# A graph layer whose fourth gather of each group takes 126 rows instead of 125

## The chip, the cores and the metric

The kernel runs on one core of a Trainium2 chip. The metric is the device time of one execution in microseconds (us). The engines of a core work side by side: TensorE (PE, with its weight loads PEld), VectorE (DVE), ScalarE (ACT), GpSimd (POOL) and SyncE (SP). Transfers are carried by 16 DMA engines; SP, ACT and POOL issue them.

## What is computed

One layer of a graph network over 12500 nodes of 64 features and 412500 edges of 32 features. The edges are sorted by receiver (`dst`), while their senders (`src`) are in no order.

```
h = relu(layernorm(x))
msg_in = concat(h[src], h[dst], edge_attr)                  # 160 wide
messages = silu(msg_in @ W1 + b1) @ W2 + b2
att      = softmax(silu(msg_in @ Wa1 + ba1) @ Wa2 + ba2)    # over all edges
aggregated = segment_sum(messages * att, dst)
x = x + (silu(concat(h, aggregated) @ Wu1 + bu1) @ Wu2 + bu2)
```

## The kernel before

**Tables.** The first phase (`gnn_kernel`, lines 90 to 313) normalises the nodes and multiplies them with the sender's and the receiver's part of the two first weight matrices. The products are kept in DRAM as two tables with a row of C = 128 floats (512 B) for each node: `ts_d` for senders, `tr_d` for receivers. An edge then needs the sum of a row of `ts_d`, a row of `tr_d` and a product of its own features.

**Groups and tiles.** `one_pass` (line 393) goes through the edges in NG = 413 groups of K = 8 tiles of EP = 125 edges; 3300 tiles hold all edges and the last four are padding. Within a tile each edge has its own partition, so partitions 125 to 127 are not used.

**The gather of senders.** `load(g)` (line 523) takes a buffer `gs` of 128 partitions x 8 x 128 floats from a pool of seven (line 161), keeps the first 125 partitions, and issues one indirect DMA on GpSimd for each tile (line 530). It reads 125 numbers of rows from one column of `src_sb` and fetches those rows of `ts_d` to partitions 0 to 124 of its eighth of the buffer. `src_full` (line 130) is the same table of row numbers with all 128 partitions; the host has padded partitions 125 to 127 with zeros. In 131 groups, the set `chosen` (every third group from 10 on), the eighth tile isn't gathered: ScalarE copies its 125 columns out of `hT` one by one (line 503) and TensorE multiplies them (line 565). That leaves 413 x 8 - 131 = 3173 gathers.

**The rest of a group.** Receivers are sorted, so a group's rows of `tr_d` lie in a window of 32 rows, loaded by SP (line 551). VectorE makes a one-hot matrix (line 555) and TensorE multiplies it and the edge features with the window (line 559). `begin(g)` adds the gathered rows (line 570) and ScalarE takes the tanh (line 573), from which VectorE forms the silu, the message and the attention logits (lines 583 to 594). Every four groups the largest logit is brought up to date. `by_node` (line 637) makes the weighted one-hot matrices, TensorE sums the messages by node (line 643), and `put` adds these sums to those kept in SBUF (lines 668 and 672) and notes the maximum they stand for (line 675).

**Order.** VectorE, ScalarE and TensorE follow the order in the code (`pin` keeps it). Loads run two groups ahead of their use. GpSimd's own order is that of the calls of `load`, with nothing else on it from the first gather to the last; each gather waits for the one eight before it, whose semaphore it shares, and for its buffer to be free. After the last group a short phase updates the nodes (from line 822).

Of the kernel before, what the change touches and what calls it, by code (L numbers as in the profile page):

```python
# [44 lines left out]
F32 = mybir.dt.float32  # L45
# [8 lines left out]
P = 128  # L54
EP = 125
# [3 lines left out]
C = 2 * U  # L59
S1 = U + 1  # L60
K = 8
# [13 lines left out]
PHASE = 1  # L75
SLOTS = (((0, 24), (24, 24)), ((48, 24), (72, 12)), ((84, 24), (108, 17)))
ROUND = 12582912.0
EPS = 1e-5
NEG = -3.0e38
BIG = 3.0e38  # L80
# [9 lines left out]
def gnn_kernel(ctx: ExitStack, tc: tile.TileContext, n_edges, x, src, src_row, dst, dst_row, first, edge,  # L90
# [73 lines left out]
    with tc.tile_pool(name="node1", bufs=1) as node1, \  # L164
# [41 lines left out]
        eps = node1.tile([P, 1], F32, name="eps")  # L206
        nc.vector.memset(eps, EPS)
        pin(nc.scalar.activation(node1.tile([P, 1], F32, name="spare"), eps, AF.Sqrt))
# [90 lines left out]
        for c, nn in chunks:  # L299
            tr = node.tile([P, CB, C], F32, name="tr")[:, :nn, :]  # L300
            for b in range(0, nn, 4):
                n = min(4, nn - b)
                pn = node_ps.tile([P, 4, C], F32, name="pn", bufs=4)
                for i in range(0, n, 2):
# [7 lines left out]
        pin(nc.scalar.dma_start(hT_d, hT))  # L312

    one_pass(tc, n_edges, locals())
    again = nc.values_load(wrong[0:1, 0:1], min_val=0, max_val=1,
                           skip_runtime_bounds_check_because="it is the outcome of a comparison")
# [76 lines left out]
def one_pass(tc, n_edges, v):  # L393
    nc = tc.nc
    NB, T, NG, NP, NT = (v[k] for k in ("NB", "T", "NG", "NP", "NT"))
    ident, iota_w, bj, dloc, src_sb, base_sb, real, unreal, far, wrong = (
        v[k] for k in ("ident", "iota_w", "bj", "dloc", "src_sb", "base_sb", "real", "unreal",
                       "far", "wrong"))
    ts_d, tr_d, bq_d, xb_d, edge, dst_row = (
        v[k] for k in ("ts_d", "tr_d", "bq_d", "xb_d", "edge", "dst_row"))  # L400
    wa2, ba2_c, w2b, wu1a, wu2h, we, gather = (
        v[k] for k in ("wa2", "ba2_c", "w2b", "wu1a", "wu2h", "we", "gather"))
# [8 lines left out]
    with ExitStack() as ctx:  # L411
# [38 lines left out]
        for w in wins:  # L450
            nc.vector.memset(w, 0.0)
            for r in range(2):
                rows = slice(WR + r * DE, WR + (r + 1) * DE)
                nc.vector.tensor_copy(w[rows, :, r, :], we[rows, None, :].to_broadcast([DE, 2, C]))
        with tc.tile_pool(name="work2", bufs=2) as work2, \
# [3 lines left out]
            pes, gss, lgs, ps_, psums, sps, pps, ees, mts, nums, cols = ({} for _ in range(11))  # L459
# [20 lines left out]
            def places(g):  # L480
# [7 lines left out]
                pin(nc.vector.tensor_scalar(near, to, 1.0 / m, 0.5 / m - 0.5, op0=ALU.mult, op1=ALU.add))  # L488
                pin(nc.vector.tensor_scalar(near, near, ROUND, None, op0=ALU.add))
                pin(nc.vector.tensor_scalar(near, near, ROUND, float(1 - m * P), op0=ALU.subtract, op1=ALU.mult))  # L490
                pin(nc.vector.scalar_tensor_tensor(to, to, float(P), near, op0=ALU.mult, op1=ALU.add))
# [13 lines left out]
            def burst(g, k):  # L505
                for i in range(EVERY):
# [6 lines left out]
                           ap=[[C, NP + WR - SHIFT], [SHIFT * C, 2], [1, C]])  # L513

            def registers(g, engine, at, base=base_sb, top=NP - 1):
                n = min(NQ, NG + (base is not base_sb) - g)
                _, regs = nc.values_load_multi_w_load_instructions(
                    base[0:1, g:g + n], engines=[engine], min_val=0, max_val=top,
                    skip_runtime_bounds_check_because=WHY)
                for i in range(n):  # L520
                    at[g + i] = regs[i]

            def load(g):

                t = g * K
                if g % NQ == 0:
                    registers(g, ENG.SP, at_sp)
                gs = gss[g] = gather.tile([P, K, C], F32, name="gs")[:EP]
                for j in range(K - (g in chosen)):
                    nc.gpsimd.indirect_dma_start(  # L530
                        out=gs[:, j, :], out_offset=None, in_=ts_d[:, :],
                        in_offset=bass.IndirectOffsetOnAxis(ap=src_sb[:, t + j:t + j + 1], axis=0))
                if g % NQ == 0:
                    n = min(NQ, NG - g) * E2
                    eo = eos[g // NQ % 2]
                    i = g // NQ % 2
                    db = dbs[i * WR:(i + 1) * WR].bitcast(I32)
                    for i in range(g, min(g + NQ, NG)):
                        e = slice((i - g) * E2, (i - g + 1) * E2)
                        ees[i] = eo[:, e], db[:, e]  # L540
                    nc.sync.dma_start(eo[WR:, :n],
                                      edge[:, g * E2:g * E2 + n])
                    for r in range(2):
                        nc.sync.dma_start(
                            db[r * R:(r + 1) * R, :n],
                            bass.AP(tensor=dst_row.tensor, offset=dst_row[r:r + 1, g * E2:].offset,
                                    ap=[[0, R], [1, n]]))
                eo, db = ees.pop(g)
                win = wins[g % WINS]
                for r in range(2):  # L550
                    nc.sync.dma_start(win[r * R:(r + 1) * R, :, r, :],
                                      tr_w[bass.ds(at_sp[g], R), :, :])
                for h in range(2):
                    e = slice(h * E2 // 2, (h + 1) * E2 // 2)
                    pin(nc.vector.tensor_scalar(eo[:WR, e], db[:, e], bj[g // NQ % 2 * WR:(g // NQ % 2 + 1) * WR, g, h:h + 1], None,  # L555
                                                op0=ALU.is_equal))
                pe = pes[g] = pre_ps.tile([P, K, C], F32, name="pe")[:EP]
                for q in range(H):
                    pin(nc.tensor.matmul(pe[:, 2 * q:2 * q + 2, :], eo[:, q * EP:(q + 1) * EP],  # L559
                                         win[:, q // 2, :, :], start=True,  # L560
                                         stop=q < H - 1 or g not in chosen))
                if g in chosen:
                    to, _ = cols[g]
                    pin(nc.vector.scalar_tensor_tensor(to, nums[g], half, to, op0=ALU.is_equal, op1=ALU.mult))
                    pin(nc.tensor.matmul(pe[:, K - 1, :], to, stack, start=False, stop=True))
# [166 lines left out]
            for g in range(AHEAD):  # L732
                load(g)
            done = 0
            for g in range(NG):
# [18 lines left out]
                if g + AHEAD < NG:  # L754
                    load(g + AHEAD)
# [382 lines left out]
```

## Time and profile before

| | |
|---|---|
| median of 3 runs | 4922.53 us (4922.45 to 4923.75) |
| the profiled execution | 4935.06 us |
| its span, first to last instruction | 4933.3 us |
| gathers (line 530) | 3173, first start 51.9 us, last start 4875.7 us |
| one gather, shortest / median / longest | 1207 / 1212 / 1726 ns |
| queue 0 (GpSimd's transfers) | 253840 packets, 206.77 MB |
| queue 1 (SP's transfers) | 121458 packets, 174.49 MB |

The profile is one execution, so sums of its durations are made against its own time, which is a little over the median of the runs. In a group's line the columns are the code line, the engine, the operation, output and inputs by the program's names, and the number of instructions; then busy time and mean duration, and the idle time of the engine just before them with what ended it. "issue" means that the engine waited for nothing the profile shows. In the view of one line, three durations stand for shortest, median and longest in ns. In the timeline the columns are start, duration, engine, line and operation, and idle time before it. A gather's duration on POOL is the time GpSimd works on it, not that of the transfer, which the DMA engines do afterwards.

### The profile page before, as it was taken

What the parts mean: (1) busy time and instruction counts of PE and PEld (TensorE: products, weight loads), DVE (VectorE), ACT (ScalarE), POOL (GpSimd) and SP (SyncE); (2) the same over time, 40 slices, a digit from 0 to 9 for tenths busy, and PEclk for the clock granted to TensorE, in tenths of its full rate; (3) what the DMA queues carried; (4) which work ended last, traced back from release to release, by engine and by line L of the source; (5) the groups of instructions that cost most, each with busy time, mean ns of one, the idle gap of its engine ahead of it and who ended that gap; (6) DMA issues with size and microseconds to landing.
All of it is one profiled execution on the core that took longest, in us unless ns stands there. A gap on an engine that the chain in (4) does not pass through costs nothing. (4 is left out here: it accounts for less than half of the span.)

```text
span 4933.3 us, 81829 instructions
## 1 busy us (share of the span) xinstructions
PE 2429.9 (49%) x11509; PEld 1950.7 (40%) x11509; DVE 3456.5 (70%) x9793; ACT 2214.0 (45%) x17625; POOL 3871.1 (78%) x3198
## 2 busy tenths in 40 slices
PE   5455555445544444544444544444445445444455
PEld 4343344334433333433333443333334334334344
DVE  6677777777776766766766776766767667667667
ACT  3444444444444444444444444444444444444412
POOL 4777877777777777777777777777777777777775
PEclk8666655665666665555665555566566666655655
DMA  7333333333333333333333333233333333333333
GB/s 248 76 76 83 87 75 82 89 74 83 81 75 76 71 74 76 70 75 76 69 76 76 68 76 76 68 76 76 69 76 71 74 76 70 75 76 70 75 91 81
DMA packets 377225, 396.20 MB, mean 80 GB/s; under 512 B 230333, under 2 KB 306039, under 8 KB 376290
## 3 DMA queue, kind: packets, MB, share of 16 engines
q0 software_dynamic: 253840, 206.77, 19.0%
q1 hardware_dynamic: 121458, 174.49, 14.9%
q10 hardware_dynamic: 1376, 9.67, 0.5%
q14 instruction: 457, 3.74, 0.3%
q8 instruction: 94, 1.54, 0.1%
HBM read 361.41 MB, written 25.72 MB: 78 GB/s over the span
## 5 line engine op out<-in xcount | busy, mean ns | idle before, releaser
L530 POOL DMA_INDIRECT gs<-ts_d,src_sb x3173 | 3853.9, 1215 | 1020.6 <-issue 962.4
L559 PE MATMUL pe<-wins,eo 128*125 128x256 f32 x3304 | 1524.4, 637 | 1551.2 <-DVE eo L555 1288.7
L503 ACT COPY cols<-hT 128x1 f32 x16375 | 1630.2, 189 | 754.3 <-issue 749.8
L559 PEld LDWEIGHTS pe<-wins,eo 128*125 128x125 f32 x3304 | 997.4, 319 | 1872.4 <-DVE eo L555 1375.5
L570 DVE TENSOR_TENSOR gs<-pe,gs 125x1024 f32<-125x1024 f32 (+1 forms) x413 | 487.5, 1180 | 1153.1 <-DMA gs<-ts_d,src_sb 1140.2
L573 ACT ACTIVATE pe<-gs 125x1024 f32<-125x1024 f32 x413 | 424.8, 1029 | 1768.2 <-DVE gs L570 859.2
L637 DVE TENSOR_SCALAR wt<-iota_w,dloc,p 125x40 f32<-125x40 f32 x3304 | 772.5, 364 | 1.8
L643 PE MATMUL sp<-wt,acts 125*65 125x40 f32 x6608 | 652.2, 270 | 13.2 <-DVE wt L637 9.2
L643 PEld LDWEIGHTS sp<-wt,acts 125*65 125x65 f32 x6608 | 612.5, 185 | 23.6 <-DVE wt L637 14.0
L613 PE MATMUL mt<-ident,mx 125*128 125x125 f32 x110 | 48.1, 438 | 644.7 <-DVE sums L672 608.1
L654 PEld LDWEIGHTS mt<-ss,w2u 65*128 65x128 f32 x826 | 210.7, 283 | 362.0 <-issue 235.4
L654 PE MATMUL mt<-ss,w2u 65*128 65x40 f32 x826 | 188.3, 322 | 262.8 <-DVE gm L620 199.4
L555 DVE TENSOR_SCALAR eo<-dbs,bj 64x250 f32<-64x250 int32 x826 | 303.2, 397 | 17.9 <-DMA dbs<-in_dst_row_dram 8.5
L591 DVE TENSOR_TENSOR pe<-pe,w_all 125x512 f32<-125x512 f32 x413 | 288.8, 699 | 13.7
L589 DVE SCALAR_TENSOR_TENSOR pe<-pe,gs 125x512 f32<-125x512 f32 x413 | 287.4, 696 | 10.8
L583 DVE SCALAR_TENSOR_TENSOR acts<-pe,gs 125x512 f32<-125x512 f32 x413 | 284.6, 689 | 12.8 <-issue 2.4
L594 DVE TENSOR_REDUCE lg<-pe 125x8 f32<-125x512 f32 x413 | 284.2, 688 | 10.8
L613 PEld LDWEIGHTS mt<-ident,mx 125*128 125x128 f32 x110 | 20.0, 182 | 655.8 <-issue 652.2
L675 DVE COPY stand<-nmax 64x40 f32 x826 | 217.1, 263 | 3.3
L672 DVE TENSOR_TENSOR sums<-sums,mt 64x40 f32 x606 | 114.4, 189 | 4.7 <-issue 0.4
L668 DVE SCALAR_TENSOR_TENSOR sums<-sums,scale,mt 64x40 f32 x220 | 55.8, 254 | 78.4 <-PE mt L654 59.6
L356 DVE TENSOR_SCALAR bu<-mt,w_all 64x256 f32<-64x256 f32 (+1 forms) x50 | 23.9, 478 | 92.6 <-PE mt L347 78.6
(124 smaller groups left out, 1123.2 us busy)
## 6 DMA issues: line engine op xcount, KB each, us to landing
eo<-in_edge_dram SPq DMA_DIRECT2D x103, 500.0 KB
dbs<-in_dst_row_dram SPq DMA_DIRECT2D x206, 250.0 KB
gs<-ts_d,src_sb POOLq DMA_INDIRECT x3173
wins<-tr_d SPq DMA_DIRECT2D x826, 32.0 KB
num<-in_src_row_dram SPq DMA_DIRECT2D x131, 62.5 KB
ts_d<-ts SPq DMA_DIRECT2D x5, 896.0 KB
tr_d<-tr ACTq DMA_DIRECT2D x5, 896.0 KB
hT_d<-hT ACTq DMA_DIRECT2D x1, 3136.0 KB
```

What stands on the lines that cost most here:

```text
L503: pin(nc.scalar.copy(to[:, first + i:first + i + 1], hT[:, bass.ds(regs[i], 1)]))
L530: nc.gpsimd.indirect_dma_start(out=gs[:, j, :], out_offset=None, in_=ts_d[:, :], in_offset=bass.IndirectOffsetOnAxis(ap=src_sb[:, t + j:t ...
L555: pin(nc.vector.tensor_scalar(eo[:WR, e], db[:, e], bj[g // NQ % 2 * WR:(g // NQ % 2 + 1) * WR, g, h:h + 1], None, op0=ALU.is_equal))
L559: pin(nc.tensor.matmul(pe[:, 2 * q:2 * q + 2, :], eo[:, q * EP:(q + 1) * EP], win[:, q // 2, :, :], start=True, stop=q < H - 1 or g not in ...
L570: pin(nc.vector.tensor_tensor(gss[g][:, :n, :], pes[g][:, :n, :], gss[g][:, :n, :], ALU.add))
L573: pin(nc.scalar.activation(pes[g], gss[g], AF.Tanh))
L583: pin(nc.vector.scalar_tensor_tensor(acts[g % ACTS][:, :, 0:U], th[:, :, U:C], 1.0, gs[:, :, U:C], op0=ALU.add, op1=ALU.mult))
L589: pin(nc.vector.scalar_tensor_tensor(att, th[:, :, 0:U], 1.0, gs[:, :, 0:U], op0=ALU.add, op1=ALU.mult))
L591: pin(nc.vector.tensor_tensor(att, att, wa2[:EP, None, :].to_broadcast([EP, K, U]), ALU.mult))
L637: pin(nc.vector.tensor_scalar(wt[:, j, :], iota_w[:EP, j // H, :], dloc[:, g * K + j:g * K + j + 1], p[:, k + j:k + j + 1], op0=ALU.is_equ ...
L643: pin(nc.tensor.matmul(sp, acts[g % ACTS][:, j, :], wt[:, j, :], start=j == 0, stop=j == K - 1))
L654: pin(nc.tensor.matmul(pp, w2u.rearrange("s h u -> s (h u)"), sps.pop(g), start=True, stop=True))
```

## The change

The constant `WIDE = 126` is new. The gather of tile 3 of each group (the fourth) now reads 126 row numbers and writes 126 partitions; the others stay at 125. The added row number lies in the padding of `src_full` and is 0, so the added row is row 0 of `ts_d`, and it lands in partition 125 of the buffer, which no later step reads. The instructions on all engines keep their number and order.

```diff
+WIDE = 126
@@ one_pass
-    ident, iota_w, bj, dloc, src_sb, base_sb, real, unreal, far, wrong = (
+    ident, iota_w, bj, dloc, src_full, base_sb, real, unreal, far, wrong = (
@@ load(g)
-                gs = gss[g] = gather.tile([P, K, C], F32, name="gs")[:EP]
+                full = gather.tile([P, K, C], F32, name="gs")
+                gs = gss[g] = full[:EP]
                 for j in range(K - (g in chosen)):
+                    rows = WIDE if j == 3 else EP
                     nc.gpsimd.indirect_dma_start(
-                        out=gs[:, j, :], out_offset=None, in_=ts_d[:, :],
-                        in_offset=bass.IndirectOffsetOnAxis(ap=src_sb[:, t + j:t + j + 1], axis=0))
+                        out=full[:rows, j, :], out_offset=None, in_=ts_d[:, :],
+                        in_offset=bass.IndirectOffsetOnAxis(ap=src_full[:rows, t + j:t + j + 1], axis=0))
```

More of the change, by code (lines that the diff above doesn't have):

```diff
@@ L395, in one_pass @@
     NB, T, NG, NP, NT = (v[k] for k in ("NB", "T", "NG", "NP", "NT"))
-    ident, iota_w, bj, dloc, src_sb, base_sb, real, unreal, far, wrong = (
-        v[k] for k in ("ident", "iota_w", "bj", "dloc", "src_sb", "base_sb", "real", "unreal",
+    ident, iota_w, bj, dloc, src_full, base_sb, real, unreal, far, wrong = (
+        v[k] for k in ("ident", "iota_w", "bj", "dloc", "src_full", "base_sb", "real", "unreal",
                        "far", "wrong"))
```

## The prediction

> **What bounds the kernel now.** I read the busy shares first, then the waits by pair of engines, then the groups of GpSimd (POOL), then GpSimd's timeline.
>
> ```profile
> PE 2429.9 (49%) x11509; PEld 1950.7 (40%) x11509; DVE 3456.5 (70%) x9793; ACT 2214.0 (45%) x17625; POOL 3871.1 (78%) x3198
> DVE gs L570 <- DMA gs<-ts_d,src_sb: 1140.2, 303, 7.9
> POOL gs L530 <- issue: 962.4, 2993, 49.5
> L530 POOL DMA_INDIRECT gs<-ts_d,src_sb x3173 | 3853.9, 1215 | 1020.6 <-issue 962.4
> ```
>
> POOL has the largest busy share, 78%. VectorE's biggest wait (total, times, longest) is for gathered rows, 1140.2 us. POOL's own idle time is nearly all "issue": it waits for nothing. So POOL turns out gathers back to back and the rest follows.
>
> ```profile
> 2126.93 1.21 POOL L530 DMA_INDIRECT gs<-ts_d,src_sb  x1 [0.30 <-issue]
> 2127.22 0.17 DVE L675 COPY stand<-nmax 64x40 f32 x1
> 2127.52 0.61 DVE L675 COPY stand<-nmax 64x40 f32 x1
> 2128.45 1.21 POOL L530 DMA_INDIRECT gs<-ts_d,src_sb  x1 [0.31 <-issue]
> 4875.68 1.21 POOL L530 DMA_INDIRECT gs<-ts_d,src_sb  x1 [0.31 <-issue]
> ```
>
> One gather is 1.212 us and 0.305 us to the next, 1.517 in all. The first starts at 51.9, the last ends at 4876.9: 4825.0 us for 3173 gathers, 1.521 each. Before them lie 51.9 us, behind them 56.4, and these make the span of 4933.3. A change of x in each of 413 gathers therefore moves the end by 413x, in either direction, as long as POOL stays the bound.
>
> The two middle copies are the second thing to see. They are the same instruction inside the same gather, 0.17 and 0.61 us long. This view (shortest/median/longest ns) shows that it is no accident:
>
> ```profile
> L675 DVE COPY stand<-nmax x826: 165/178/617, 151.5 to 4892.9; 64x40 f32 x166
> L672 DVE TENSOR_TENSOR sums<-sums,mt x606: 175/194/202, 168.2 to 4838.9; 64x40 f32 x152
> ```
>
> Sorted by when they start within a gather, copies of L675 that start up to 0.56 us after the gather take 0.18; those that start between 0.58 and about 1.0 all end at 1.193; later ones take 0.17 again. So in each gather POOL holds something that the copy needs, for 617 - 171 = 446 ns, from about 0.57 to 1.02; the longest copies of L637 and L555 are stretched by 457 and 424. L672, which has a PSUM operand, is never held. I read a gather as 0.57 us of preparation, 0.445 us in which the descriptors are written to SBUF, and 0.19 us to finish.
>
> **What one gather writes.** From the queue row:
>
> ```profile
> q0 software_dynamic: 253840, 206.77, 19.0%
> ```
>
> 253840 / 3173 = 80 packets for each gather. By size, the trace's packets are 15 of 4096 B, 5 of 512 B, 33 of 32 B and 27 of 4 B. The first two kinds are five equal shares of 25 rows (three packets of eight 512 B rows, and one row). The others fit eleven more DMA engines that get the same pattern in 4 B pieces (3 x 32 B and 1 x 4 B), and sixteen 4 B writes at the end, one for each engine. So sixteen lists advance in step, each by 25 + 1 = 26 places, though eleven hold nothing of use. Five is the largest number up to 16 that cuts 125 into equal shares.
>
> The page "DMA: Bandwidth & Descriptors" of the Trainium skill (section "Why a DMA increments its semaphore by 16 and not by 1") gives this as a rule, the largest k up to 16 that divides the slowest dimension; the five shares agree with it, and it would make 14 of 126.
>
> **The change part by part.**
>
> *126 rows.* Cut equally in the same way, 126 rows make 14 shares of 9: 10 places per list in place of 26. If the 445 ns go by places (17.1 ns each), the wide gather's writing takes 171 ns and the gather 1212 - 274 = 938 ns. All 413 groups keep their fourth tile (3173 = 413 x 8 - 131: where a tile is left out, it is the eighth). 413 x 0.274 = 113.2 us less, all on POOL's chain. This is the value I take, since the 445 ns are the one stretch of a gather that a row ties to the writing.
>
> Its bounds: no shape but 125 rows is gathered here, so the split of a gather into fixed and growing parts is open. If the preparation goes by places too, (1212 - 190) x 16/26 = 629 ns go, 260 us in all: 4662. If nothing goes, 0. A loss is possible too: see the first rival.
>
> *The extra row.* 413 more rows of 512 B, always row 0 of the table: 0.2 MB of 206.77. By rows, 1212 / 125 = 9.7 ns, 4.0 us in all, if generation goes by rows and not by places.
>
> *Transfers.* Shares of 9 rows instead of 25 land sooner. That is worth nothing: gathers are issued up to seven buffers ahead, and the DMA engines are busy about three tenths. The waits of a gather (its own semaphore, eight gathers back; its buffer) are unchanged, and POOL hardly waits for them now.
>
> *Other engines.* Instructions and order are the same on all of them. VectorE has 1140.2 / 413 = 2.76 us of waiting for rows in each group, against 0.27 (at most 0.63) that the change would give; it doesn't become the bound. The port is held 274 ns less in one gather of eight, so a few copies get shorter, under that same cover. The last group lands as before, so the 56.4 us of tail stay.
>
> *Sum.* The profiled execution took 4935.06, span 4933.3: 4935.1 - 113.2 = 4821.9. The median of the runs is 4922.53, 12.5 lower; I put the forecast against that: 4922.5 - 113.2 = **4809.3 us** (-2.3%).
>
> A rule speaks against it: the same page (section "Anatomy of one DMA — SWDGE (gpsimd) path") calls descriptor generation small, and says that many descriptors can be emitted before the cost shows. The row has 1212 ns of POOL for 125 rows, which isn't small, but doesn't say what part grows. By the rule the sum would be 4922.5.
>
> **The rivals.**
>
> *Slower: POOL pays by engines that get real rows.* Each real share may need work of its own (a start address, a queue pointer), while the empty lists are filled cheaply. Then 14 shares in place of 5 cost nine times that price. If the 445 ns are five shares of 89, the wide gather is 801 ns longer: 413 x 0.801 = 331 us, 5253. If only the closing 0.18 us goes by shares (36 each), it is 320 ns: 132 us, 5055. It decides once a share costs more than 274 / 9 = 30 ns. For it: five real shares are few, and a kernel with more of them is nowhere in the trace. Against it: the eleven empty lists are written out to the same length, which looks like one step over all sixteen.
>
> *No difference.* The 445 ns could be the reading of 125 indices, or a fixed block, and generation could go by rows: +4.0 us, 4926.5. The change may also not do what I read into it: if the 126th row is put behind five shares of 25, the lists have 27 places, 413 x 17 ns = +7 us, 4929.6. Both lie within 0.2% (9.8 us), about what a measurement of this kernel can tell from no change.
>
> *A gain that is lost on VectorE* would need it to lack the 2.76 us per group; excluded above.
>
> **How the numbers follow.** Forecast and its bounds (4662 to 4912): 0.57. No difference: 0.12. Slower: 0.31, of which I put some 0.13 below 5060. The range from 4660 to 5060 then leaves out the dearer part of the slower rival and holds about 0.82. The likeliest case by itself: 4660 to 4912. Faster by over 0.2%: 0.57; within: 0.12; slower: 0.31.
>
> **What would show it.** In the changed profile every eighth gather should take about 0.94 us and the others 1.212, with 0.305 between; POOL busy about 3871 - 113 = 3758. The packets of queue 0 should fall by 413 x (80 - 48), about 13200: 14 x 2 for the rows, 2 x 2 on the two empty lists, 16 closing writes. Copies stretched by a wide gather should be stretched by at most some 0.17 us. VectorE's wait for rows should fall by about the gain. I am wrong if the wide gather is 1.2 us or longer, if the packets show another split, or if a wait for rows grows although POOL got shorter.

## The result and the profile after

The changed kernel takes 4832.97 us (median of 4 runs, 4832.67 to 4833.29), the one before 4922.49. The ratio is 0.9818, with an interval of 0.9801 to 0.9835: 89.5 us less, where 113.2 were forecast (4809.3). The kernel before ran again beside each batch of experiments: it took 4923 to 4932 us there, but 4968 beside e12 and e11, whose times are disturbed, so that only the durations of their gathers are used. Times given "on 4922.5" are the measured ratio put on that time.

Here are the rows of the changed kernel's page and waits that answer to those shown of the kernel before. Line 533 is now the gather, 573 the addition of gathered rows, 678 the copy that was line 675.

```profile
PE 2424.5 (50%) x11509; PEld 1945.6 (40%) x11509; DVE 3435.4 (71%) x9793; ACT 2202.4 (46%) x17625; POOL 3770.8 (78%) x3198
DVE gs L573 <- DMA gs<-ts_d,src_sb: 1053.4, 292, 8.4
POOL gs L533 <- issue: 957.7, 2983, 48.6
L533 POOL DMA_INDIRECT gs<-ts_d,src_sb x3173 | 3753.7, 1183 | 1018.5 <-issue 957.7
q0 software_dynamic: 240624, 206.55, 19.3%
```

POOL is busy 3770.8 us instead of 3871.1 and still waits for hardly anything but "issue". VectorE's wait for rows fell by 86.8, about what was gained: its slack took the whole change, as it should where POOL is the bound. The timeline of POOL shows where:

```profile
2000.90 1.21 POOL L533 DMA_INDIRECT gs<-ts_d,src_sb  x1 [0.30 <-issue]
2002.41 1.00 POOL L533 DMA_INDIRECT gs<-ts_d,src_sb  x1 [0.30 <-issue]
2003.71 1.21 POOL L533 DMA_INDIRECT gs<-ts_d,src_sb  x1 [0.30 <-issue]
```

The middle row is the wide gather. Sorted by tile in the trace, the fourth takes 996 ns (median of 413), each of the others 1209, with 305 between as before. 413 x (1209 - 996) = 88.0 us, within 2 us of the measured 89.5. The two spans differ by more, 4933.3 - 4831.0 = 102.3, because the profiled execution of the kernel before was itself 12.6 us over its median: there the gathers of 125 rows took 1212 ns, here 1209, and 2760 x 3 ns are 8 us.

Queue 0 lost 253840 - 240624 = 13216 packets, 32 for each wide gather: 80 became 48. Their sizes in the trace make a wide gather of 14 packets of 4096 B, 14 of 512 B, 2 of 32 B and 18 of 4 B, which fits fourteen shares of 8 + 1 rows, two lists without rows and sixteen closing writes.

### The profile page after: what moved, and what is told of

It reads as the page before. It is cut to its first block, busy times and chain, and to the rows that moved or that the text cites. A ratio compares the mean times of both kernels' runs of the same rounds, so it can differ in the third digit from the quotient of the medians.

```text
span 4831.0 us, 81829 instructions
## 1 busy us (share of the span) xinstructions
PE 2424.5 (50%) x11509; PEld 1945.6 (40%) x11509; DVE 3435.4 (71%) x9793; ACT 2202.4 (46%) x17625; POOL 3770.8 (78%) x3198
## 3 DMA queue, kind: packets, MB, share of 16 engines
q0 software_dynamic: 240624, 206.55, 19.3%
## 5 line engine op out<-in xcount | busy, mean ns | idle before, releaser
L533 POOL DMA_INDIRECT gs<-ts_d,src_sb x3173 | 3753.7, 1183 | 1018.5 <-issue 957.7
```

The source lines that it names most:

```text
L533: nc.gpsimd.indirect_dma_start(out=full[:rows, j, :], out_offset=None, in_=ts_d[:, :], in_offset=bass.IndirectOffsetOnAxis(ap=src_full[:ro ...
```

## The experiments

What was to be told apart: does POOL's time for a gather go by the rows of one share (the theory, "places"), by lists that hold no rows (the rival that the same two points allow), or is it not POOL's time at all but the sooner landing of rows spread over more engines? All edits are to the changed kernel unless another is named.

**e4_sizes**: the kernel before with one more gather for each group, in sixteen sizes.

```diff
+ROWS = (128, 127, 124, 123, 122, 121, 120, 117, 112, 110, 108, 96, 75, 64, 32, 16)
@@ load(g), ahead of the group's own gathers
+                rows = ROWS[g % 16]
+                nc.gpsimd.indirect_dma_start(
+                    out=v["extra"].tile([P, C], F32, name="ex")[:rows], out_offset=None, in_=ts_d[:, :],
+                    in_offset=bass.IndirectOffsetOnAxis(ap=v["src_full"][:rows, t:t + 1], axis=0))
```

> The kernel before (all its gathers of 125 rows) with one more gather for each group, into a buffer that nobody reads, of 128, 127, 124, 123, 122, 121, 120, 117, 112, 110, 108, 96, 75, 64, 32 or 16 rows in turn. The kernel before and the change give two points: 1212 ns with 26 places in each list, 996 ns with 10. Theory (places): a gather takes 861 + 13.5 x places ns, with places = rows of one equal share + 1 and as many shares as the largest number up to 16 that divides the rows. So 128 rows 983 ns, 127 rows (one share) 2589, 124 (4 x 31) 1293, 123 (3 x 41) 1428, 122 (2 x 61) 1698, 121 (11 x 11) 1023, 120 983, 117 (13 x 9) 996, 110 (11 x 10) 1010, 108 (12 x 9) 996, 96 955, 64 928, 16 888; 5528 us in all. Rival (empty lists): what costs is each list without rows, (1212 - 996) / 9 = 24 ns, on a base of 948. So 128, 112, 96, 64, 32 and 16 rows all 948, 127 rows 1308, 124 1236, 123 1260, 122 1284, 121 and 110 1068, 117 1020, 108 1044; 5485 us in all. Rival (more than 125 rows is a cheaper path): 128 and 127 near 996, all others 1212 or a little less.

It took 5506.7 us. The extra gathers ran early, from 50 to 996 us, about 25 of each size. This row of their line has shortest, median and longest:

```profile
L532 POOL DMA_INDIRECT ex<-ts_d,src_sb x413: 853/980/2570, 50.1 to 995.9; - x138
```

Medians by size, in order of the rows in one share:

| rows | shares x rows | ns | places | empty lists |
|---|---|---|---|---|
| 16 | 16 x 1 | 857 | 888 | 948 |
| 32 | 16 x 2 | 884 | 902 | 948 |
| 64 | 16 x 4 | 935 | 928 | 948 |
| 75 | 15 x 5 | 927 | 942 | 972 |
| 96 | 16 x 6 | 931 | 955 | 948 |
| 112 | 16 x 7 | 960 | 969 | 948 |
| 128 | 16 x 8 | 956 | 983 | 948 |
| 120 | 15 x 8 | 984 | 983 | 972 |
| 117 | 13 x 9 | 980 | 996 | 1020 |
| 108 | 12 x 9 | 992 | 996 | 1044 |
| 110 | 11 x 10 | 993 | 1010 | 1068 |
| 121 | 11 x 11 | 1012 | 1023 | 1068 |
| 124 | 4 x 31 | 1295 | 1293 | 1236 |
| 123 | 3 x 41 | 1412 | 1428 | 1260 |
| 122 | 2 x 61 | 1682 | 1698 | 1284 |
| 127 | 1 x 127 | 2555 | 2589 | 1308 |

The number of rows says little: 124 rows take longer than 126, and 127 more than twice as long. The rows of one share say nearly all: over a range of 857 to 2555 ns the column "places", the theory's, is never off by more than 34. The rival with empty lists fails by over 1200 ns at 127, and no other price saves it: from 122 to 127 rows one more list is empty (15 instead of 14), and the time grows by 873 ns. The rival that a gather wider than 125 rows is cheaper fails at 127 as well. Nor is it the number of packets: gathers of 16, 64 and 120 rows make 32 each and take 857, 935 and 984 ns. The sizes of all 281200 packets of the run are those that these shares make. The whole time, 5506.7, lies midway between the sums of the theory and of the empty lists (5528 and 5485) and decides nothing, since the gathers of 125 rows changed too (1202 ns at the median). Between 128 and 127 rows the slope is (2555 - 956) / 119 = 13.4 ns for each row of a share.

**e10_shares**: the same with other sizes, to see whether the number of shares matters at equal length.

```diff
-ROWS = (128, 127, 124, 123, 122, 121, 120, 117, 112, 110, 108, 96, 75, 64, 32, 16)
+ROWS = (128, 120, 104, 88, 72, 112, 105, 98, 91, 77, 80, 75, 70, 65, 55, 125)
```

> The kernel before with one more gather for each group into a buffer that nobody reads, of 128, 120, 104, 88, 72 rows (8 rows in each of 16, 15, 13, 11, 9 shares), 112, 105, 98, 91, 77 (7 rows in 16, 15, 14, 13, 11), 80, 75, 70, 65, 55 (5 rows in 16, 15, 14, 13, 11) and 125. Theory (rows of one share alone): the same time within some 10 ns at each length: 984, 970 and 927 ns; with sixteen shares 28 to 40 ns less, as seen with 128, at all three lengths. Rival (each empty list costs): a rise with each share that is missing, 24 ns by the first two points, so 72 rows 144 ns above 120. 125 rows: 1212.

(72 was put in the wrong row: it divides into 12 shares of 6.) The medians again: with 8 rows in a share 986, 981, 982 and 972 ns for 16, 15, 13 and 11 shares. With 7 rows: 937, 951, 958, 951, 958 for 16 down to 11. With 5 rows: 914, 919, 937, 919, 937. At one length the time moves by at most 23 ns, where 24 for each empty list would make 120. 72 rows took 950 as 12 x 6, and 125 rows 1186. The 28 to 40 ns that sixteen shares should save at all three lengths were missed: 28 ns less than fifteen at 8 rows in e4, but here 5 more at 8 rows, 14 less at 7 and 5 less at 5.

**e1_four_wide and e2_all_126**: four wide gathers in each group, and all.

```diff
-                    rows = WIDE if j == 3 else EP
+                    rows = WIDE if j % 2 else EP      # e1
+                    rows = WIDE                       # e2
```

> 126 rows in tiles 1, 3, 5 and 7 of each group: 413 x 3 + 282 = 1521 wide gathers instead of 413. Theory (the gain is POOL's time and POOL stays the bound): 4922.5 - 1521 x 0.2165 = 4593 us. Rival (the gain came from rows landing sooner, which one wide gather of a group already gives, or VectorE is soon the bound): well above 4593, between 4700 and 4833.

> 126 rows in all 3173 gathers. Theory, if POOL stays the bound: 4922.5 - 3173 x 0.2165 = 4236 us. VectorE waits 1053 us for rows after the change and 596 us more would go, so POOL should just stay the bound on average, but groups differ, and where VectorE is the slower one the gain is cut: 4236 to 4400. Rival (rows landing sooner): near the change, 4833.

The ratio to the kernel before is 0.9338 (0.9323 to 0.9354) for e1 and 0.8625 (0.8610 to 0.8639) for e2; on 4922.5 that is 4597 and 4246 us, for 4593 and 4236 expected. The gain grows in step with the number of wide gathers, from 413 to 1521 to 3173. A gain by sooner landing would have been used up with the first. These are rows of e2's page, its waits and its lines:

```profile
PE 2411.1 (57%) x11509; PEld 1937.3 (46%) x11509; DVE 3326.9 (78%) x9793; ACT 2200.9 (52%) x17625; POOL 3191.9 (75%) x3198
DVE gs L573 <- DMA gs<-ts_d,src_sb: 571.5, 260, 7.4
L533 POOL DMA_INDIRECT gs<-ts_d,src_sb x3173: 992/999/1312, 51.4 to 4193.8; - x199
L678 DVE COPY stand<-nmax x826: 165/177/408, 138.1 to 4211.0; 64x40 f32 x166
```

VectorE's share, 78%, has now passed POOL's 75%, and yet POOL is the bound: its gathers follow one another at 1306 ns from first to last (999 + 305), and VectorE still waits 571.5 us for rows. The busy share leaves out the 305 ns between gathers; the waits don't. The last row is of the copies that POOL holds up: the longest is 408 ns, so it was held for 408 - 171 = 237, where it was 446 with 125 rows.

**e6_giveback**: put a little work on POOL behind each wide gather and see whether the time comes back.

```diff
+                    if j == 4:
+                        nc.gpsimd.memset(pad, 0.0)      # pad is 128 x 64
```

> The change, with a memset of 128 x 64 on POOL behind each wide gather. Theory (the gain is POOL's time): the time rises by 413 times what the memset adds on POOL, 0.1 to 0.5 us with its gap, so 4874 to 5040 us, and by the trace's own figure within 10 us. Rival (rows landing sooner, or any gain outside POOL): stays near 4833.

The experiment missed: nothing ties the memset to its place, and all 413 ran between 2.3 and 177.5 us, 289 of them ahead of the first gather.

```profile
L535 POOL MEMSET pad<- x413: 152/152/942, 2.3 to 177.5; 128x64 f32 x138
L536 POOL DMA_INDIRECT gs<-ts_d,src_sb x3173: 992/1210/1733, 65.3 to 4821.1; - x199
```

The gathers began at 65.3 us instead of 51.0, and at 150 us they stood still for 26.8. That is 41 us, and its ratio of 0.9902 (0.9885 to 0.9918) makes 4874 on 4922.5, 41 more than the change (4880.2 as measured). It says that POOL's start is on the path, not what it was built for.

**e8_giveback_in_order**: the same, with gathers and memsets kept in the order of the code.

```diff
-                        nc.gpsimd.memset(pad, 0.0)
+                        pin(nc.gpsimd.memset(pad, 0.0))
-                    nc.gpsimd.indirect_dma_start(
+                    pin(nc.gpsimd.indirect_dma_start(
```

> The change, with the memset of 128 x 64 now held in its place behind each wide gather (in the earlier run all 413 of them ran before and among the first gathers, 152 ns each and 209 from one to the next). Theory (the gain is POOL's time): the memsets stand in POOL's row of gathers and give back 209 ns each, 413 x 0.209 = 86 us, so 4919 us, nearly the time of the kernel before; 4896 to 4960 with other gaps around them. Rival (rows landing sooner, or any gain outside POOL): stays near 4833.

The ratio is 0.9868 (0.9852 to 0.9884), 4857.5 on 4922.5: 24.5 us more than the change, not 86. The timeline of POOL tells why:

```profile
2004.49 1.00 POOL L536 DMA_INDIRECT gs<-ts_d,src_sb  x1 [0.30 <-issue]
2005.49 0.17 POOL L535 MEMSET pad<- 128x64 f32 x1
2005.83 1.35 POOL L536 DMA_INDIRECT gs<-ts_d,src_sb  x1 [0.17 <-issue]
2007.49 1.21 POOL L536 DMA_INDIRECT gs<-ts_d,src_sb  x1 [0.31 <-issue]
```

The memset lies inside the time between two gathers, which grows from 305 to 347 ns; the next gather grows by 11 at the median, 13 in the mean (this one by more). 413 x (42 + 13) = 23 us, which is what came back to within 2 us. So the price that I expected was wrong, by my taking the 305 ns for POOL's own work; that POOL's row of gathers sets the end holds.

**e9_wide_127**: the same tile, one row more.

```diff
-WIDE = 126
+WIDE = 127
```

> The change with 127 rows instead of 126 in the fourth tile. 127 has no divisor up to 16 but 1, and took 2555 ns as an extra gather. Theory (places, POOL bound): 4922.5 + 413 x (2.555 - 1.2095) = 5478 us, slower by 11%. Rival (a wider gather than 125 is cheaper, or more engines and not shorter lists): no slower than the kernel before.

The ratio is 1.113 (1.1112 to 1.1149), 5479 on 4922.5, for 5478 expected. In POOL's timeline the gather that took 1.00 us with 126 rows takes 2.55:

```profile
2008.21 1.21 POOL L533 DMA_INDIRECT gs<-ts_d,src_sb  x1 [0.30 <-issue]
2009.72 2.55 POOL L533 DMA_INDIRECT gs<-ts_d,src_sb  x1 [0.30 <-DVE eo L558]
2012.58 1.21 POOL L533 DMA_INDIRECT gs<-ts_d,src_sb  x1 [0.30 <-issue]
```

A gather of 127 rows makes 15 packets of 4096 B and one of 3584 B (127 rows in one list) and, on fifteen other lists, 15 of 32 B and one of 28 B each: 127 places with nothing in them. That is the clearest sight of lists that are all of one length; whether they are written side by side or in turn the times don't tell. The copies that POOL holds up show the same length. The longest was held for 1962 - 171 = 1791 ns, 1345 more than with 125 rows, and 102 places more make 13.2 ns for each:

```profile
L678 DVE COPY stand<-nmax x826: 165/178/1962, 161.8 to 5436.3; 64x40 f32 x166
```

**e12_one_128, e11_alternate and e13_one_128_again**: 128 rows in the fourth tile; 126 and 128 in turn; and the first of these again.

```diff
-WIDE = 126
+WIDE = 128                                            # e12, e13
-                    rows = WIDE if j == 3 else EP
+                    rows = WIDE + j % 2 * 2           # e11, with WIDE = 126
```

> The change with 128 rows instead of 126 in the fourth tile. A gather of 128 rows took 944 ns where all had 128 rows, and 956 and 983 as an extra gather among others. Theory (rows of one share alone): 8 rows, about 983, so 4833 - 413 x 0.013 = 4828 us. Rival (sixteen shares have a shorter path of their own): 944 to 956 here too, so 4833 - 413 x 0.046 = 4814 us.

> 126 and 128 rows in turn, in all gathers. If sixteen shares have a shorter path of their own, the 128s take 944 to 956 and the 126s 997, and the time lies halfway between all 126 and all 128, about 4170 us. If it is the run of equal gathers that makes them short, the 128s take about 983 and the time is about 4228.

> The kernel with 128 rows in the fourth tile once more, on its own. Its first run took 5260 us although its wide gathers took only 957 ns: ScalarE's column copies of line 504 waited 2120 us for nothing that the profile shows, instead of 736. If that belongs to the kernel (128 rows between gathers of 125), it comes back: 5200 or more, with the same idle time on ScalarE. If it belonged to the chip and the time of that run (the kernel before took 4968 there, 45 us more than elsewhere), it goes: 4833 - 413 x (0.996 - 0.957) = 4817 us, beside a kernel before near 4923.

e12 took 5260 us and e11 6043, against every theory here. Their gathers were short all the same, 957 ns for 128 rows in e12, 960 and 1001 for 128 and 126 in e11. In both, ScalarE's column copies stood still instead (3125.1 us of "issue" in e11). The first row is from the waits of e12, the second from those of e13:

```profile
ACT cols L504 <- issue: 2119.6, 3839, 2.3
```

```profile
ACT cols L504 <- issue: 740.2, 1034, 1.7
```

e13 is e12's kernel on another chip: 4817.9 us, ratio 0.9787 (0.9771 to 0.9803), for 4817 expected, and the wait is gone. So e12's time wasn't the kernel's; e11 wasn't run again. What held ScalarE up isn't known. The durations answer the question: among gathers of 125 rows (957) and of 126 (960), sixteen shares of 8 are shorter than 983, so most streams show a saving of about 25 ns for sixteen shares, and e10 doesn't.

**e3_all_128 and e7_tiles_128**: all gathers with 128 rows; and tiles of 128 edges, so that the rows are of use.

```diff
-WIDE = 126
+WIDE = 128
-                    rows = WIDE if j == 3 else EP
+                    rows = WIDE
-EP = 125                                              # e7 alone
+EP = 128
-SLOTS = (((0, 24), (24, 24)), ((48, 24), (72, 12)), ((84, 24), (108, 17)))
+SLOTS = (((0, 24), (24, 24)), ((48, 24), (72, 12)), ((84, 24), (108, 20)))
```

> 128 rows in all 3173 gathers (three rows go to partitions that aren't used). Theory (places): 9 places, 983 ns, 13.5 less than with 126 rows: 4922.5 - 3173 x 0.229 = 4194 us if POOL is still the bound, up to 4400 where VectorE is. Rival (empty lists): 948 ns, 4085 us.

> Tiles of 128 edges instead of 125, all gathered with 128 rows: 403 groups and about 3096 gathers. Theory (places), if POOL is the bound: 3096 x (0.983 + 0.305) + 107 = 4095 us. If VectorE has become the bound, its work falls with the number of groups, so 403 / 413 of what 128 rows in tiles of 125 give, 2.4% less. Rival (empty lists): 948 ns, 3986 us.

e3: ratio 0.8304 (0.8290 to 0.8317), 4088 us as measured; e7: 0.8100 (0.8087 to 0.8114), 3989 us, the fastest version here and faster than both kernels. Each lies about 105 us below the theory's figure and within 3 us of the rival's. That is chance: a gather of 128 rows takes 944 ns here, close to the rival's 948, but e4 and e10 exclude what the rival is built on. The last gather of e3's line starts at 4023.6 and a gather follows another at 1253 ns, so POOL is still the bound:

```profile
L533 POOL DMA_INDIRECT gs<-ts_d,src_sb x3173: 940/944/1370, 50.4 to 4023.6; - x199
DVE gs L573 <- DMA gs<-ts_d,src_sb: 385.5, 193, 6.8
```

Of the 983 - 944 = 39 ns that the theory lacks, sixteen shares would make some 25, as in e12 and e13; the rest isn't explained. The copies of line 678 show where to look:

```profile
L678 DVE COPY stand<-nmax x826: 165/177/427, 137.5 to 4040.7; 64x40 f32 x166
```

The longest is held for 427 - 171 = 256 ns, more than the 237 with 126 rows, though each list is a place shorter. But the hold begins sooner: copies are held from 0.52 us after the start of a gather, and from 0.57 with 125 and 126 rows. So what sixteen shares save lies outside the hold, some 50 ns of it ahead; what GpSimd does less there no run shows.

## Why the prediction was right, and where its size was off

*POOL is the bound, and x in each of 413 gathers moves the end by 413x.* Right. The gain follows the number of wide gathers through e1 and e2, and e9 shows the same in the other direction.

*126 rows make 14 shares of 9, with 10 places instead of 26.* Right, by the packets (48 as forecast) and by e4 and e9, where 127 rows make one share. That all lists are of one length is seen; that they advance in step, as the prediction has it, isn't. The rule for the number of engines in the Trainium skill (page "DMA: Bandwidth & Descriptors", section "Why a DMA increments its semaphore by 16 and not by 1") holds for all the sizes tried: the packets of e4 and e10, size by size, are those that it makes.

*17.1 ns for each place, 274 ns in all.* This is the term that was mis-sized. Measured are 13.4 ns, and 213 to 217 ns for 16 places. The prediction let all 445 ns in which POOL holds VectorE's copies go by places. With 126 rows the hold is 237 ns, so the 16 places take 209 ns of it, and about 100 ns of the hold don't go by places (the same comes out with 127 rows). 413 x 0.217 is 89.6 instead of 113.2.

*The preparation of 0.57 us doesn't go by places; at the bound it does, and 260 us go.* The value taken was right and the bound not needed. In e2, with 126 rows throughout, copies start to be held 0.57 us after the start of a gather, as with 125, and the gather's time fell by about as much as the hold (213 and 209 ns).

*A copy should be stretched by at most some 0.17 us in a wide gather.* It is 0.24, for the same reason.

*The extra row costs nothing that matters.* Right: 128 rows are cheaper than 125. Queue 0 even moved 0.2 MB less in place of 0.2 MB more, since the empty lists are shorter.

*The first rival, a price for each engine with real rows.* Wrong: fourteen and sixteen shares are cheaper than five, and at equal length the number of shares moves a gather by at most 23 ns (e10). What I held against it, the empty lists written out to the same length, was the right reason.

*No difference.* Wrong. The sentence of the same page (section "Anatomy of one DMA — SWDGE (gpsimd) path") that many descriptors can be emitted before the cost shows doesn't hold for these gathers: 16 places fewer show as 213 ns of 1209.

*A gain lost on VectorE.* Excluded rightly, and by far: even with 944 ns in all gathers VectorE waits 385.5 us for rows.

## What to carry to other kernels

Where GpSimd issues indirect gathers back to back, choose the number of rows by the length of one share: 126 or 128 rows, which cut into 14 and 16 equal shares, are cheaper than 125, which cut into 5, and 127 is the worst of the sizes tried. Only rows of 512 B were tried. A row that goes to waste can be the cheapest way to a better cut. Look at the packets' sizes for the cut, and at another engine's stretched instructions for the part of an instruction that grows with it.

## What the runs showed of the hardware that was not expected

GpSimd holds up VectorE's copies in each gather, for up to 446 ns with 125 rows, 237 with 126 and 1791 with 127, while an addition of the same shape with a PSUM operand is never held (202 ns at most before, 203 after); whether the operand or the kind of operation spares it wasn't tested. A memset of 172 ns fits almost wholly between two gathers: the 305 ns there are not all POOL's work, and it costs 55 ns. Gathers in sixteen shares were about 25 ns or more shorter than the theory's figure in most runs, though not in e10. And on one chip ScalarE's copies waited nearly three times as long for nothing that the profile shows (2119.6 us), in the same kernel that waited 740.2 on another; e8, e9 and e10 have 1073 to 1430 us of the same wait. Its cause stays open.
